# Newton's products in other slots: a two-layer non-local block on one core

## The chip, the cores and the metric

The kernel runs on one core of a Trainium2 chip. The metric is the device time of one execution in microseconds (us); three runs of the kernel before are shown with their median. TensorE is called PE here, its weight loads PEld, VectorE DVE, ScalarE ACT, GpSimd POOL and SyncE SP, as in the profile.

## The reference

Two layers of the same kind are applied to four images of 128 channels and 96 x 96 pixels, all in float32. With `C = 128` and `CI = 64`, one layer is:

```python
g_x = maxpool2(conv1x1(x, g_w, g_b)).reshape(b, CI, -1).transpose(0, 2, 1)
theta_x = conv1x1(x, theta_w, theta_b).reshape(b, CI, -1).transpose(0, 2, 1)
phi_x = maxpool2(conv1x1(x, phi_w, phi_b)).reshape(b, CI, -1)
attn = jax.nn.softmax(jnp.einsum('bqc,bck->bqk', theta_x, phi_x), axis=-1)
y = jnp.einsum('bqk,bkc->bqc', attn, g_x).transpose(0, 2, 1).reshape(b, CI, H, W)
W_y = conv1x1(y, W_w, W_b)
inv = bn_gamma * jax.lax.rsqrt(bn_var + BN_EPS)
return W_y * inv[None, :, None, None] + (bn_beta - bn_mean * inv)[None, :, None, None] + x
```

Each image has 9216 queries and 2304 keys.

## The kernel before, in words

**Slots and cycles.** There are eight blocks (an image and a layer), in the order of `ORDER`: image 0 layer 0, image 1 layer 0, image 0 layer 1, image 2 layer 0 and so on. A block's queries come in nine pairs of 1024. The keys come in 18 tiles of 128, and a slot `t` of the main loop takes two of them: nine slots are a pair, 18 slots (`CYCLE`) are a cycle, and the whole is 648 slots, 0 to 647. Within a cycle a slot is called by its number `s = t % 18`.

**What one slot issues, in this order.** The scores of the first key tile (L929: eight PE instructions of 512 columns, one for each of four 64 x 64 tiles of the array and two passes) and its exponential on ScalarE (L934); then a step called *first*, if the slot has one; the scores and exponential of the second key tile; then a step called *second* (in the tables below the main loop: *middle*); the additions of both exponentials to the row sums on VectorE (L943), between them what takes a product out of PSUM; then the products with the values for the slot before (L951, sixteen instructions); then a step that *closes* the slot; last what hangs on tails (pools, the fold of the row sums: L1023 to L1030, called the turn) and on `after` (small preparation steps). All queues are in order, and the order is this program's.

**The work beside the attention.** In cycles in which the next block's keys are made (0 to 7, 9 to 16, 18 to 25 and 27 to 30) eight slots (s = 8, 9, 11, 12, 14, 17 and 2, 5 of the next cycle) have a *stage*: a product for g, phi and theta of the next block (`Unit`), as *first*, with a sum on VectorE. Slots 3 and 13 have the projection of a finished pair (`multiply`: L1105, or L1098 where it is folded; L1116 and L1124 or L1136 take it out), slots 1 and 10 of cycles 1 to 3 a theta product (L906, L914), slot 4 after an odd unit a mix. All of these, and Newton's products, use the same two PSUM banks (`two_banks`), so a product waits until what it finds there has been read. `is_free(t)` says that a slot has none of the others.

**Newton's products.** `Fold` computes two 64 x 64 matrices B, one for each layer, by 14 Newton steps. The raw weights are transposed (`steps_raw`: four steps of four 32 x 32 transposes, L171), squared and summed (`squares`: L319, L320), and `scale` (L332) and `init` make the start. A step is `half` (a product L353 into PSUM, from which VectorE makes V, L359) and `whole` (a product L375 with V, from which ScalarE makes the next X, L379). After the 14 steps there are two rounds of `product` (L391) and `residual` (L403; L409 subtracts on VectorE); the first makes B, the second mends it, and the last residual is what a check reads. `steps_last` then notes the residual and the growth and turns the result into layer 1's last weights. Pairs from number 9 on use B in their projection, from slot 103.

Before, `scale` and `init` stand in slot 16, Newton's steps in the free slots from 18 on, and each slot holds a whole step: `half` as *first* or, where the slot before closed with one, as *middle*, and `whole` as the close. The last residual stands in slot 69, `steps_last` in slots 70 to 76.

The small tiles of `Fold` lie in `spare`, one of three buffers for an image. Image index 2 (the third) is later loaded into that buffer by six DMAs on SP, in slots 97, 104, 115, 122, 133 and 140; its first readers stand in slot 164.

Of the kernel before, what the change touches and what calls it, by code (L numbers as in the profile page):

```python
# [33 lines left out]
NP = HW // PT  # L34
KB = 2
NB = NKT // KB
# [10 lines left out]
STORE = 3  # L47
DRAIN = 15
MIX = 22


FOLDS = (8, 9, 11, 12, 15), (17, 18, 20, 21, 24)
# [7 lines left out]
CYCLE = 2 * NB  # L60
# [8 lines left out]
def shifted_blocks(ctx: ExitStack, tc: tile.TileContext, x: bass.AP, layers, out: bass.AP, flag):  # L69
# [24 lines left out]
    nc = tc.nc  # L94
# [23 lines left out]
    ones = const.tile([P, CI], F32, name="ones")  # L118
# [173 lines left out]
    class Fold:  # L292
# [146 lines left out]
        def steps(self):  # L439

            low, todo = NEWTON_LOW, []
            for k in range(NEWTON):
                c = 2.0 / (1.0 + low * (2.0 - low))
                low *= c * (2.0 - low)
                todo += [self.half(k), self.whole(k, c)]
            right = lambda: self.raw[:, CI:]
            todo += [self.product("first", right, self.first), self.residual]
            todo += [self.product("mended", lambda: self.rest, self.mended), self.residual]
            return todo

        def steps_last(self):

            w = ws[1]

            def both():
                nc.scalar.copy(self.M[:CI, :], ident[:CI, :CI])
                for step in turned(self.M[CI:, :], self.B[1][:CI, :]):
                    step()

            def scaled():  # L460
                nc.vector.tensor_scalar(self.M_bn, self.M, w.inv, None, ALU.mult)

            return [self.note, self.note_growth, both, scaled] + turned_twice(w, self.M_bn)
# [829 lines left out]
    def then(t, step):  # L1293
        after[t] = after.get(t, []) + [step]

    fold = Fold()
# [14 lines left out]
    then(9, lambda: ws[1].load_gphi((nc.sync, nc.sync)))  # L1311
    then(9, lambda: ws[1].load_theta(nc.sync))
    for i, step in enumerate(fold.steps_raw()):
        then((14, 14, 15, 15)[i], step)
    then(15, fold.keys_side)
    then(15, fold.squares)
    slow = [CYCLE + i // len(PREPARE) * CYCLE + PREPARE[i % len(PREPARE)] for i in range(11)]
    parts_of(ws[1], "gphi", slow[:4])
    parts_of(ws[1], "theta", slow[4:6])
# [25 lines left out]
    for n in range(1, len(blocks)):  # L1345
        for u in (1, 3):
            mixes[(n - 1) * NP * NB // CYCLE * CYCLE + u * CYCLE + MIX] = (n, u)
    loads = {
        5 * CYCLE + 7 + i // 2 * CYCLE + i % 2 * 7: (2, i) for i in range(6)
    } | {  # L1350
        14 * CYCLE + 14 + (i + 1) // 2 * CYCLE - i % 2 * 7: (3, i) for i in range(6)
    }
# [6 lines left out]
    def is_free(t):  # L1359
        q, s = 2 * (t // CYCLE), t % CYCLE  # L1360
        return not (
            t in stages or t in mixes or t in keys or t - 1 in keys or t in (THETAS, THETAS + 1)
            or (0 < q < NP - 1 and s in ALONE) or (q and s in PROJECT)
        )

    firsts, middles, closes = {}, {}, {}
    todo, t = fold.steps(), CYCLE
    middles[CYCLE - 2], closes[CYCLE - 2] = fold.scale, fold.init
    while todo:
        if is_free(t):  # L1370
            (middles if t - 1 in closes else firsts)[t] = todo.pop(0)
            closes[t] = todo.pop(0)
        t += 1
    for i, step in enumerate(fold.steps_last()):
        then(t + i, step)
    assert t + i + 1 < min(loads)

    gone, pending = [], (None, None)
    for t in range(total + 1):
# [8 lines left out]
        if t in keys:  # L1388
            n, i = keys[t]
# [19 lines left out]
        if t < total:  # L1409
# [12 lines left out]
            if t in loads:  # L1422
                b, i = loads[t]
# [335 lines left out]
def nonlocal_blocks(tc: tile.TileContext, x: bass.AP, layers, out: bass.AP):  # L1759
    with tc.tile_pool(name="flag", bufs=1) as pool:  # L1760
        flag = pool.tile([1, 1], I32, name="flag")
        shifted_blocks(tc, x, layers, out, flag)
        bad = tc.nc.values_load(flag[0:1, 0:1])
        with tc.If(bad > 0):
            general_blocks(tc, x, layers, out)
# [30 lines left out]
```

## Time and profile before

| what | us |
|---|---|
| median of three runs | 2479.27 |
| lowest and highest of them | 2479.05, 2481.05 |
| the profiled execution | 2479.74 |
| its span, first to last instruction | 2477.9 |
| PE busy | 2455.1 (99%) |
| DVE busy | 2073.5 (84%) |
| ACT busy | 1695.8 (68%) |
| POOL busy | 901.3 (36%) |

The mean granted clock of TensorE is 0.997. A row of a timeline has start, duration, engine, line, operation, tiles and count, and in brackets the engine's idle time before it with what ended it. Rows of the groups have busy time and mean ns behind the first bar, idle time behind the second. Rows of the waits have the total, the number and the longest. Rows of the windows have the length, then the busy time of PE, PEld, DVE, ACT and POOL, then the granted clock, the DMA share and GB/s. Matmuls overlap and their ends are modelled, so the distance of starts says more than the duration.

### The profile page before, as it was taken

Reading aid. Unit: us, or ns where it says so; the run is one execution under the profiler, and the core shown is the slowest. Engines: PE = TensorE matmul, PEld = TensorE weight load, DVE = VectorE, ACT = ScalarE, POOL = GpSimd, SP = SyncE. Lnnn points to the kernel's source line nnn. Section 1 sums busy time; section 2 is a strip of 40 time slices with the busy share of each in tenths; the row PEclk is TensorE's granted clock in tenths of the full one; section 3 lists DMA queues with packets and bytes.
Section 4 is the critical chain, followed back from the end, with each engine's and each line's share of the span. In section 5 each row is a group of like instructions: output and inputs, shape, how many; then the busy total and the mean of one; then the engine's idle time right before and its main releaser. Section 6 shows DMA issues by size and latency. Waiting matters only on the chain.

```text
span 2477.9 us, 59287 instructions
## 1 busy us (share of the span) xinstructions
PE 2455.1 (99%) x23627; PEld 1133.7 (46%) x23627; DVE 2073.5 (84%) x2671; ACT 1695.8 (68%) x1928; POOL 901.3 (36%) x1033
## 2 busy tenths in 40 slices
PE   9899999999999999999999999999999999999999
PEld 3344444454444444444444444444444444444444
DVE  8888898888788888888878888888887888887777
ACT  6566666667767667666666767677666676776666
POOL 0222332443243443434434344443433444322331
PEclk9999999999999999999999999999999999999999
DMA  5455556677467776767656677676745677644443
GB/s 189 78 91 92 99 108 130 124 141 132 81 99 132 121 135 128 138 131 140 116 101 110 124 129 134 119 137 112 123 80 99 119 125 129 126 88 86 85 87 65
DMA packets 199629, 283.95 MB, mean 115 GB/s; under 512 B 36262, under 2 KB 131888, under 8 KB 199344
## 3 DMA queue, kind: packets, MB, share of 16 engines
q0 software_dynamic: 101872, 137.69, 42.1%
q1 hardware_dynamic: 97304, 142.31, 20.1%
q8 instruction: 188, 3.08, 0.5%
q14 instruction: 97, 0.79, 0.1%
q10 hardware_dynamic: 168, 0.07, 0.0%
HBM read 54.07 MB, written 35.68 MB: 36 GB/s over the span
## 4 chain that ended last, share of the span: by engine, by line
PE 92%; DVE 4%; DMA 1%; issue 1%; ACT 0%; POOL 0%; DVEq 0%; SPq 0%; POOLq 0%; ACTq 0%
PE sc L929 43%; PE av L951 43%; PE unit_ps L693 4%; DVE sum L943 2%; PE W_ps L1098 1%; DMA sums<-x 1%; PE gphi_ps L550 1%; PE unit_ps L702 0%; DMA turned<-sum 0%; PE W_ps L1105 0%; ACT exp L934 0%; DMA sum<-turned 0%; PE mix_ps L852 0%; PE theta_ps L906 0%; DMA x<-in_x_dram 0%
## 5 line engine op out<-in xcount | busy, mean ns | idle before, releaser
L934 ACT ACTIVATE exp<-sc,nshift 128x1024 f32<-128x1024 f32 x1296 | 1400.3, 1113 | 702.0 <-PE sc L929 646.3
L943 DVE TENSOR_TENSOR sum<-sum,exp 128x1024 f32<-128x1024 f32 x1151 | 1406.6, 1222 | 300.2 <-ACT exp L934 249.2
L929 PE MATMUL sc<-theta,phi 64*64 64x512 f32 x10224 | 1533.7, 590 | 0.0
L951 PE MATMUL av<-exp,gT 64*64 64x512 f32 x10368 | 1443.0, 590 | 0.0
L929 PEld LDWEIGHTS sc<-theta,phi 64*64 64x64 f32 x10224 | 554.5, 133 | 582.3 <-issue 536.4
L951 PEld LDWEIGHTS av<-exp,gT 64*64 64x64 f32 x10368 | 542.3, 133 | 582.2 <-issue 539.6
L662 POOL DMA_DIRECT2D sums<-x x252 | 344.1, 1863 | 408.5 <-PE unit_ps L693 245.3
L1003 POOL DMA_DIRECT2D turned<-sum x140 | 115.3, 943 | 653.0 <-DMA turned<-sum 441.9
L1016 POOL DMA_DIRECT2D sum<-turned x280 | 266.5, 1729 | 118.1 <-DMA sum<-turned 115.5
L1120 POOL DMA_DIRECT2D x<-halves x122 | 109.0, 1107 | 246.8 <-ACT halves L1116 224.1
L693 PE MATMUL unit_ps<-sums,mixed 64*64 64x384 f32 x896 | 178.6, 486 | 0.2 <-DMA sums<-x 0.2
L1129 POOL DMA_DIRECT2D x<-halves x122 | 163.5, 1883 | 0.3 <-issue 0.3
L941 DVE TENSOR_TENSOR sum<-exp,exp 128x1024 f32<-128x1024 f32 x72 | 88.1, 1224 | 42.2 <-ACT exp L934 42.1
L1085 POOL DMA_DIRECT2D halves<-halves x70 | 98.4, 1406 | 0.3 <-issue 0.2
L958 ACT COPY halves<-av 128x1024 f32<-128x1024 f32 x71 | 71.9, 1013 | 32.9 <-PE av L951 31.3
L693 PEld LDWEIGHTS unit_ps<-sums,mixed 64*64 64x64 f32 x896 | 64.6, 133 | 55.1 <-issue 35.5
L693 PE MATMUL unit_ps<-x,mixed 64*64 64x384 f32 x448 | 86.4, 485 | 0.0
L1124 ACT ACTIVATE halves<-W_ps,ends 128x256 f32<-128x256 f32 x122 | 62.3, 560 | 2.0
L1098 PE MATMUL W_ps<-halves,fold 64*64 64x256 f32 x488 | 58.2, 376 | 0.0
L693 PE MATMUL unit_ps<-sums,gphiT 64*64 64x384 f32 x224 | 55.4, 493 | 0.7 <-DMA sums<-x 0.7
L662 POOL DMA_DIRECT2D sums<-sums x28 | 23.2, 830 | 81.7 <-PE unit_ps L702 38.9
L1116 ACT ACTIVATE halves<-halves,ends 128x512 f32<-128x512 f32 x61 | 49.4, 810 | 0.0
(194 smaller groups left out, 1103.8 us busy)
## 6 DMA issues: line engine op xcount, KB each, us to landing
sums<-x POOLq DMA_DIRECT2D x252, 192.0 KB, 5.8
x<-halves POOLq DMA_DIRECT2D x244, 128.0 KB, 4.6
sums<-x SPq DMA_DIRECT2D x112, 192.0 KB
turned<-sum SPq DMA_DIRECT2D x140, 128.0 KB
turned<-sum POOLq DMA_DIRECT2D x140, 128.0 KB, 3.9
halves<-halves POOLq DMA_DIRECT2D x70, 256.0 KB, 5.2
halves<-row SPq DMA_DIRECT2D x140, 128.0 KB
out_dram<-x SPq DMA_DIRECT2D x35, 512.0 KB
```

What stands on the lines that cost most here:

```text
L662: return lambda: nc.gpsimd.dma_start(out=dst(), in_=src(), accum_op=ALU.add)
L693: nc.tensor.matmul(bank[ts(c, CI), :UN], lhsT=lhsT, rhs=rhs[:, c, :], start=True, stop=True)
L929: nc.tensor.matmul(ps[ts(c, CI), ts(h, QT)], lhsT=self.blk.keys_of(k, c, h), rhs=self.th[ts(h, CI), :], start=True, stop=True,)
L934: nc.scalar.activation(e, ps, AF.Exp, bias=nshift)
L941: nc.vector.tensor_add(self.sum, self.es[0], e)
L943: nc.vector.tensor_add(self.sum, self.sum, e)
L951: nc.tensor.matmul(self.av[ts(h, CI), ts(r, QT)], lhsT=self.blk.gT[ts(r, CI), k, :], rhs=e[ts(r, CI), ts(h, QT)], start=(k == 0), stop=(k ...
L1003: nc.gpsimd.dma_start(out=self.turned[ts(h, CI)], in_=self.sum[ts(h, CI), ts(h, QT)], accum_op=ALU.add,)
L1016: nc.gpsimd.dma_start(out=folded()[ts(i, SQ)], in_=self.turned[ts(i, SQ), ts(k, n)], accum_op=ALU.add,)
L1085: nc.gpsimd.dma_start(out=self.y, in_=self.halves[:, QT:], accum_op=ALU.add)
L1120: nc.gpsimd.dma_start(out=here[:CI, h, :], in_=top[ts(h, CI), :], accum_op=ALU.add)
L1129: nc.gpsimd.dma_start(out=here[CI:, :, ts(c, n)], in_=self.y[ts(c, CI), :].rearrange("p (h n) -> p h n", h=2), accum_op=ALU.add,)
```

## The change

`steps_raw` moves from slots 14, 14, 15, 15 to 16, 17, 18, 19; `keys_side` and `squares` from 15 to 20; `scale` and `init` to slot 22. Newton's steps follow in the free slots from 24. `half` is always *middle* now. Where the slot is number 6 or 15 of a cycle (`APART`), `whole` is the *first* of the next slot, 7 or 16; elsewhere it closes the same slot. This gives the steps slots 24/25, 33/34, 36, 42/43, 51/52, 54, 58, 60/61, 69/70, 72, 73, 78/79, 82 and 87/88; the first check (`first`, `residual`) has slot 90 and the second (`mended`, `residual`) slot 91. In slot 94 a product of one column by one (`together`) with 128 rows is new. `steps_last` moves to slots 95 to 101. The loads of image index 2 move by a cycle, to slots 115, 122, 133, 140, 151 and 158.

```diff
+APART = (6, 15)
...
+        def together(self):
+            self.begin("together")
+            nc.tensor.matmul(
+                self.pss[0][:1, :1], lhsT=ones[:, :1], rhs=ones[:, :1], start=True, stop=True
+            )
...
-        then((14, 14, 15, 15)[i], step)
-    then(15, fold.keys_side)
-    then(15, fold.squares)
+        then(16 + i, step)
+    then(20, fold.keys_side)
+    then(20, fold.squares)
...
-        5 * CYCLE + 7 + i // 2 * CYCLE + i % 2 * 7: (2, i) for i in range(6)
+        6 * CYCLE + 7 + i // 2 * CYCLE + i % 2 * 7: (2, i) for i in range(6)
...
-    todo, t = fold.steps(), CYCLE
-    middles[CYCLE - 2], closes[CYCLE - 2] = fold.scale, fold.init
+    todo, t = fold.steps(), CYCLE + 4
+    middles[t], closes[t] = fold.scale, fold.init
     while todo:
+        t += 1
         if is_free(t):
-            (middles if t - 1 in closes else firsts)[t] = todo.pop(0)
-            closes[t] = todo.pop(0)
+            middles[t] = todo.pop(0)
+            if t % CYCLE in APART:
+                t += 1
+                assert is_free(t)
+                firsts[t] = todo.pop(0)
+            else:
+                closes[t] = todo.pop(0)
+    assert t < (NP + 2) * NB + 4
+    while not is_free(t + 1):
         t += 1
+    firsts[t + 1] = fold.together
     for i, step in enumerate(fold.steps_last()):
-        then(t + i, step)
-    assert t + i + 1 < min(loads)
+        then(t + 2 + i, step)
+    assert t + i + 3 < min(loads)
```

## The prediction

> **What bounds the kernel now.** I read the page first, then TensorE's timeline slot by slot, then the waits of the stretch in which something besides matmuls shows.
>
> ```profile
> PE 2455.1 (99%) x23627; PEld 1133.7 (46%) x23627; DVE 2073.5 (84%) x2671; ACT 1695.8 (68%) x1928; POOL 901.3 (36%) x1033
> ```
>
> TensorE (PE) is the bound, so a change pays only where PE stands still. Full speed comes from two neighbouring rows; the next fence has them, with the starts of slots 16, 18 and 76 and the largest hole.
>
> ```profile
> 80.96 1.90 PE L929 MATMUL sc<-theta,phi 64*64 64x512 f32 x16
> 90.02 0.27 PE L332 MATMUL fold_ps_scale<-x_spare,ones 64*64 64x2 f32 x2 [7.17 <-DVE x_spare L320]
> ...
> 98.88 1.12 PE L929 MATMUL sc<-x_spare,phi 64*64 64x512 f32 x8
> ...
> 111.25 1.90 PE L929 MATMUL sc<-x_spare,phi 64*64 64x512 f32 x16
> 112.96 1.04 PE L1105 MATMUL W_ps<-halves,WT 64*64 64x512 f32 x8
> ...
> 340.56 0.59 PE L929 MATMUL sc<-theta,phi 64*64 64x512 f32 x1
> ```
>
> Sixteen matmuls of 512 columns take 112.96 - 111.25 = 1.71 us, 0.107 each; I scale other widths by columns. A slot without extras (32 such) is 3.43 us, one with a stage (8 of 384 more) 4.08, one with eight more of 512 is 4.29. Next, the groups of PE from slot 16 to slot 75, with their counts:
>
> ```profile
> L951 PE MATMUL av<-exp,gT 64*64 64x512 f32 x961 | 119.4, 597 | 0.0
> L929 PE MATMUL sc<-theta,phi 64*64 64x512 f32 x816 | 107.5, 596 | 0.0
> L929 PE MATMUL sc<-x_spare,phi 64*64 64x512 f32 x144 | 18.6, 591 | 0.0
> L693 PE MATMUL unit_ps<-sums,mixed 64*64 64x384 f32 x108 | 17.4, 489 | 0.0
> L693 PE MATMUL unit_ps<-x,mixed 64*64 64x384 f32 x52 | 8.6, 501 | 0.0
> L1105 PE MATMUL W_ps<-halves,WT 64*64 64x512 f32 x56 | 8.1, 595 | 1.0 <-DVE stage L792 1.0
> L906 PE MATMUL theta_ps<-x,thetaT 64*64 64x512 f32 x48 | 6.4, 589 | 0.0
> ...
> L375 PE MATMUL fold_ps_half<-x_spare 64*64 64x64 f32 x112 | 5.1, 232 | 4.9 <-DVE x_spare L359 4.7
> L693 PE MATMUL unit_ps<-sums,gphiT 64*64 64x384 f32 x24 | 4.9, 482 | 0.0
> ```
>
> 2025 of 512 columns (217.2 us), 184 of 384 (14.8), 112 of 64 and small groups left out here (3.8) make 235.8 us of work. The stretch lasts 340.56 - 80.96 = 259.6. So 23.8 us are lost there, and this is all that the change can reach directly. They split so: slots 16 and 17 last 98.88 - 80.96 = 17.92 for 3.43 + 4.08 of work: 10.4 lost. The projection of slot 75 (L1105) waits for L792: 1.0 by its row, 1.5 with the second bank that waits behind the first (estimate). What is left, 11.9, stands in Newton's slots 18 to 70; the waits of weight loads and of PE in that stretch name the main ones:
>
> ```profile
> PEld fold_ps_half L375 <- DVE x_spare L359: 11.8, 8, 3.3
> ```
>
> ```profile
> PE unit_ps L702 <- DVE x_spare L409: 1.4, 1, 1.4
> ```
>
> The second product of a step (L375) waits for the update V (L359), which stands in VectorE's queue behind row sums, pools and the fold's turn. Everywhere a late VectorE is what PE waits for.
>
> **The change, part by part.** VectorE is a queue, so I walk it with durations from its timeline:
>
> ```profile
> 81.23 1.72 DVE L171 STREAM_TRANSPOSE x_spare<-x_spare 32x32 f32<-32x32 f32 x8
> 82.98 2.56 DVE L943 TENSOR_TENSOR sum<-sum,exp 128x1024 f32<-128x1024 f32 x2
> 85.45 0.44 DVE L1023 STREAM_TRANSPOSE turned<-sum 128x256 f32<-128x256 f32 x1
> ...
> 87.24 1.75 DVE L171 STREAM_TRANSPOSE x_spare<-x_spare 32x32 f32<-32x32 f32 x8
> ...
> 98.05 0.55 DVE L774 TENSOR_TENSOR stage<-stage,unit_ps 128x384 f32<-128x384 f32 x1
> ...
> 100.03 1.22 DVE L943 TENSOR_TENSOR sum<-sum,exp 128x1024 f32<-128x1024 f32 x1
> 101.16 0.22 DVE L267 TENSOR_TENSOR x_spare<-x_spare 128x64 f32<-128x64 f32 x1
> ...
> 102.18 0.47 DVE L359 SCALAR_TENSOR_TENSOR x_spare<-fold_ps_half,ident 64x64 f32<-64x64 f32 x2
> ...
> 106.79 0.69 DVE L914 TENSOR_TENSOR theta<-theta,theta_ps 128x512 f32<-128x512 f32 x1 [0.36 <-ACT theta L923]
> ...
> 108.53 0.68 DVE L1090 TENSOR_TENSOR halves<-halves 128x512 f32<-128x512 f32 x1
> ...
> 111.61 1.14 DVE L792 SCALAR_TENSOR_TENSOR stage<-unit_ps,cols_first,stage 128x384 f32<-128x384 f32 x2
> ```
>
> So two additions take 2.47 (82.98 to 85.45), one before other work 1.13 (100.03 to 101.16), the turn 1.79 (85.45 to 87.24), one step of `steps_raw` 0.87 (half of 1.75), stage 5's sums 1.98, `make_shift` 1.0, V 0.47, L914 0.6, L1090 0.6, a pool about 0.5 (estimate, a little under L774).
>
> *Raw transposes, squares, first product moved (slots 14-16 to 16-22).* Gone: the 10.4 of slots 16 and 17, that is the wait of 7.17 and 3.2 of slow running behind it. What comes: without the eight transposes at 81.23 VectorE begins slot 15's additions there, and after 2.47 + 1.79 slot 16's at 85.5, 4.5 behind the slot's start. Slot 16 adds 2.47 + 0.5 + 0.87 against 3.43 of PE (4.95 behind), slot 17 1.13 + 1.98 + 1.13 + 1.0 + 0.87 against 4.08 (7.0), slot 18 1.13 + 0.5 + 0.87 against 3.43 (6.1). In slot 19 L914 then ends 6.1 + 1.13 + 0.69 = 7.9 after the start; it frees the banks of slot 20's stage, due at 4.29 + 0.86 = 5.15. PE waits 2.8. The rest of slot 19 (addition, L1090, pool, two steps of four transposes) leaves VectorE 7.5 behind slot 20; with one addition and L792 it frees the banks for slot 21's W at 9.75, due at 4.08 + 2.8 + 1.72 = 8.6: 1.2 more. New cost 4.0. Bounds: 0 if VectorE catches up unseen, 7.2 if the hole merely moves. The squares are ready before slot 22; ScalarE's six copies end about when slot 21's exponentials start, hidden by the same wait.
>
> *Products apart in slots 6 and 15 of a cycle.* The first now follows both scores, so it no longer meets banks held by the slot before; the second comes after the next slot's first scores, so V has 1.72 + 0.86 instead of 1.72, and stands ahead of the turn, not behind it. The rows for slots 42 and 34:
>
> ```profile
> 169.22 0.34 PE L375 MATMUL fold_ps_half<-x_spare 64*64 64x64 f32 x8 [0.78 <-DVE x_spare L359]
> 198.13 1.22 PE L929 MATMUL sc<-theta,phi 64*64 64x512 f32 x8
> ...
> 202.91 0.34 PE L375 MATMUL fold_ps_half<-x_spare 64*64 64x64 f32 x8 [0.66 <-DVE x_spare L359]
> ```
>
> V lets L375 go 4.78 after slot 42's start. The new due time is 3.54 + 0.86 = 4.40: 0.35 left there, the same at slot 79 (like slot 43 it follows an odd unit's transposes), 0.15 at slot 25; 0.85 together, between 0 and today's wait. Slots 33/34, 51/52, 60/61, 69/70, 87/88: VectorE is earlier, 0.
>
> *The others (both products in one slot, the second at its end).* In slot 0 of a cycle V follows stage 5's sums. VectorE no longer gets the breathing space that slot 34's wait (0.78 by PE's row, about 1.1 against full speed) and slot 33's (0.5) give it today; it arrives later by that at slot 36. I take 1.2 there (bounds 0 and 1.6), 0.35 each at 54 and 72, 0.2 at 90. Slots 58, 73, 82: 0.
>
> *One check a slot, ended in slot 91.* The second residual's subtraction queues behind two additions and L1090, about 5.9 after slot 91's start; the next slot's stage needs its bank at 4.5. Cost 1.4, which is what L702 waits for L409 today, so that wait moves rather than goes. (0 to 2.0.)
>
> *`steps_last` from slots 70-76 to 95-101.* Same VectorE work; slot 75's 1.5 goes, slot 102 may get 0.4 (0 to 1.5).
>
> *The 128-row product.* Rows at such borders:
>
> ```profile
> 18.25 1.46 PE L550 MATMUL gphi_ps<-x,gphiT 128*64 128x512 f32 x6
> 19.63 1.09 PE L929 MATMUL sc<-theta,phi 64*64 64x512 f32 x8
> ...
> 2463.15 2.01 PE L951 MATMUL av<-exp,gT 64*64 64x512 f32 x16
> 2465.09 0.64 PE L969 MATMUL den_last_ps<-sum,ones 128*32 128x256 f32 x8
> ```
>
> Six matmuls of 0.214 are 1.28, the next starts after 1.38: 0.1 for leaving. Sixteen of 1.71 and the 0.12 by which tiles lag leave 0.1 for entering. With the product itself 0.3 (0.2 to 0.5). It levels the four tiles; what is queued behind it, slot 94's second scores and stage 95, keeps its order.
>
> *Image 3 a cycle later.* Six DMAs on SP of 768 KB move from slots 97-140 to 115-158: two leave a cycle with unit sums, two enter cycle 8, which has none; nothing else is queued with them that PE reads there. The tile's first reader is in slot 164. 0 (plus or minus 1.2).
>
> **Sum.** 4.0 + 0.85 + 2.1 + 1.4 + 0.4 + 0.3 = 9.05 new against 23.8 lost now: 14.75 saved. The profiled execution took 2479.74 (span 2477.9), so 2464.99; the median of the runs shown is 0.47 lower: 2464.5.
>
> **Rivals.** *A slow clock behind slot 20.* After the 7.17 us hole the granted clock fell:
>
> ```profile
> 82.00:90.00 8.00, 0.85 (x8) 0.00 (x0) 7.37 (x24) 2.29 (x7) 0.00 (x0) 0.74 0.02 3
> 90.00:96.00 6.00, 5.98 (x34) 3.21 (x38) 3.80 (x8) 1.69 (x5) 0.00 (x0) 0.50 0.14 45
> ```
>
> The clock (0.74, 0.50) stands before the last two columns. My 2.8 us hole lies below 7.17 and above 0.78, which did no harm. If it trips the clock, 3.2 more: 2467.7. The Trainium skill (TensorE: Matmul & The Clock Gate, Part 1) has the clock halved after an idle window of about 3.4 us, and a busy one of that length to lift it. By that rule 2.8 is too short, and 6 us at 0.50 are longer than the rule allows; the sum by it stays 2464.5.
>
> *The products do not profit.* If VectorE is late again by as much, Newton's slots keep 11.9 - 1.75 (slot 62's part) = 10.1, and new are 4.0 + 1.4 + 0.4 + 0.3: 16.2 against 23.8, so 2471.7. For it speaks VectorE's 84%; against it that V overtakes the turn.
>
> *Levelled tiles save the wait of every unit cycle.* Over the whole run:
>
> ```profile
>   ACT halves L1124: 18.7, 45
> ```
>
> Weights of the fifth product group wait for ScalarE's L1124, two banks a cycle, 0.42 each by this row; the second starts inside the first's shadow, so about 0.3 a cycle reaches PE (estimate). If level tiles avoid it in the 23 cycles with units behind slot 94, 7 more are saved: 2457.5. Against: ScalarE's own time ends it, and that does not move.
>
> *Slower.* The single 128-row product leaves the tiles in a state in which every later group of four 512-column matmuls takes longer. 553 slots of eight groups: at 3.3 ns a group the gain is gone, from 4.5 ns on the kernel is slower by over 0.2%; at 6 ns it takes 2491. Against: slot 21 (the 111.25 row) comes after the prologue's 128-row products, and a group takes 1.71 / 4 = 0.428 there, as everywhere.
>
> **How the numbers follow.** Forecast 0.65 (its own range 2461.5 to 2467.5), slow clock 0.10, no profit 0.12, levelled 0.08, slower or nothing 0.05. Leaving out the last two and small tails, the range is 2460 to 2472. About 0.2% (5 us) is what a measurement can tell from no change: faster 0.93, same 0.04, slower 0.03.
>
> **What would show it.** No 7 us hole before L332 and clock 1.0 around 90 us; L693 waiting about 2.8 for L914 near slot 20; L375 waiting under 3 in all; L693 waiting 1.4 for L409 behind the last check; slots after 94 as long as before. Wrong if VectorE's lag at slots 17 to 21 is much above 7.5, or if cycles from 6 on change length.

## The result, and the profile after

| | before | after |
|---|---|---|
| median, us (five runs each) | 2479.05 | 2465.37 |
| lowest and highest | 2477.76, 2481.05 | 2464.49, 2467.10 |
| the profiled execution, and its span | 2479.74, 2477.9 | 2464.86, 2462.7 |
| mean granted clock | 0.997 | 1.000 |

The ratio is 0.9945 with a 95% interval of 0.9931 to 0.9960: 13.7 us faster, against a forecast of 2464.5. In the code after, lines of `Fold` stand one line further down and those behind `together` (L454) seven further down: V is L360, the second product L376, the scores L936, the stages L700, the pair's projection L1112, `theta_alone`'s sum L921.

First the page's line of engines, of after:

```profile
PE 2450.6 (100%) x23629; PEld 1153.6 (47%) x23629; DVE 2072.2 (84%) x2671; ACT 1694.0 (69%) x1928; POOL 901.1 (37%) x1033
```

VectorE's work is the same. TensorE's idle time shrank, from 22.8 us (2477.9 - 2455.1) to 12.1, and its busy time by 4.5. About 3 of these are the slow running behind the hole: eight scores take 1.98 us at a clock of 0.50 (the row of e2 below) and 1.04 at 1.00. The windows of after at the place of the old hole (clock ahead of the last two columns):

```profile
82.00:90.00 8.00, 8.00 (x80) 2.91 (x76) 7.58 (x15) 4.85 (x5) 0.94 (x1) 1.00 0.31 61
90.00:96.00 6.00, 6.00 (x60) 2.14 (x56) 5.81 (x16) 4.88 (x6) 0.00 (x0) 1.00 0.28 76
```

PE is busy for 14.00 of 14 us at a clock of 1.00; before it was busy for 6.83 of them, at 0.74 and 0.50. Then PE's timeline from slot 20 (95.76) to the scale in slot 22:

```profile
95.76 1.04 PE L936 MATMUL sc<-x_spare,phi 64*64 64x512 f32 x8
96.62 0.80 PE L700 MATMUL unit_ps<-sums,mixed 64*64 64x384 f32 x2
99.48 0.55 PE L700 MATMUL unit_ps<-sums,mixed 64*64 64x384 f32 x3 [2.06 <-DVE theta L921]
...
105.20 1.18 PE L1112 MATMUL W_ps<-halves,WT 64*64 64x512 f32 x5 [0.56 <-DVE stage L799]
...
109.54 0.22 PE L333 MATMUL fold_ps_scale<-x_spare,ones 64*64 64x2 f32 x2
```

The scale product no longer waits, and the two new waits stand where the queue's walk had put them. VectorE's rows of after show the lag itself, at the first additions of slots 16, 18, 19 and 20 (which start at 80.53, 88.04, 91.47 and 95.76):

```profile
85.10 2.54 DVE L950 TENSOR_TENSOR sum<-sum,exp 128x1024 f32<-128x1024 f32 x2
...
95.02 1.23 DVE L948 TENSOR_TENSOR sum<-exp,exp 128x1024 f32<-128x1024 f32 x1
...
97.61 1.22 DVE L950 TENSOR_TENSOR sum<-sum,exp 128x1024 f32<-128x1024 f32 x1
...
103.39 1.22 DVE L950 TENSOR_TENSOR sum<-sum,exp 128x1024 f32<-128x1024 f32 x1
```

Last, the waits of PE and of weight loads from 80 to 480 us (total, number, longest), of after; the third fence has PE's own wait for V in before, from slot 16 to slot 75:

```profile
PE unit_ps L700 <- DVE theta L921: 2.1, 1, 2.1
PE unit_ps L700 <- DVE x_spare L410: 1.0, 1, 1.0
PE W_ps L1112 <- DVE stage L799: 0.6, 1, 0.6
PE fold_ps_half L354 <- DVE stage L785: 0.4, 1, 0.4
```

```profile
...
PEld fold_ps_half L376 <- DVE x_spare L360: 5.4, 6, 1.0
...
```

```profile
PE fold_ps_half L375 <- DVE x_spare L359: 4.7, 4, 2.5
```

L376's weights waited 11.8 before, 3.3 at most, and now 5.4, 1.0 at most; most of it lies beside PE's other work. In PE's own rows the wait for V was 4.7, and after has none. Where the time went is best seen by stretches. For each slot I take the distance between the starts of its first scores and of the next slot's, less the work in it at full speed (about 0.1073 us for 512 columns, a 32nd of a plain slot). The level of the sums hangs on the last digit of that price, the differences between before and after hardly do. The sums, in us, of these profiles:

| lost in slots | before | after |
|---|---|---|
| 16 to 75 | 23.95 | 6.92 |
| 76 to 103 | -0.17 | 2.46 |
| 104 to 143 | 3.19 | 1.84 |
| 144 and on | 6.66 | 7.32 |

So 14.4 of the 15.2 by which the span fell come from slots 16 to 103, the rest from the next 40 slots and from small differences of single executions on either side.

### The profile page after: what moved, and what is told of

Read it like the earlier page. It is cut to its first block, busy times and chain, and to the rows that moved or that the text cites. A ratio compares the mean times of both kernels' runs of the same rounds, so it can differ in the third digit from the quotient of the medians.

```text
span 2462.7 us, 59291 instructions
## 1 busy us (share of the span) xinstructions
PE 2450.6 (100%) x23629; PEld 1153.6 (47%) x23629; DVE 2072.2 (84%) x2671; ACT 1694.0 (69%) x1928; POOL 901.1 (37%) x1033
## 4 chain that ended last, share of the span: by engine, by line
PE 95%; DVE 3%; DMA 1%; issue 1%; ACT 0%; POOL 0%; DVEq 0%; POOLq 0%; SPq 0%; ACTq 0%
PE sc L936 44%; PE av L958 44%; PE unit_ps L700 4%; DVE sum L950 1%; PE W_ps L1105 1%; PE gphi_ps L557 1%; PE unit_ps L709 0%; DMA turned<-sum 0%; PE W_ps L1112 0%; DMA sums<-x 0%; DMA sum<-turned 0%; PE mix_ps L859 0%; DVE gT L875 0%; ACT exp L941 0%; PE theta_ps L913 0%
## 5 line engine op out<-in xcount | busy, mean ns | idle before, releaser
L936 PE MATMUL sc<-theta,phi 64*64 64x512 f32 x10224 | 1521.8, 589 | 0.0
L936 PEld LDWEIGHTS sc<-theta,phi 64*64 64x64 f32 x10224 | 561.3, 133 | 570.5 <-issue 518.7
L958 PEld LDWEIGHTS av<-exp,gT 64*64 64x64 f32 x10368 | 548.8, 133 | 570.2 <-issue 518.0
L669 POOL DMA_DIRECT2D sums<-x x252 | 339.0, 1825 | 391.6 <-PE unit_ps L700 227.2
L700 PE MATMUL unit_ps<-sums,mixed 64*64 64x384 f32 x896 | 177.5, 485 | 3.7 <-DVE theta L921 2.1
L700 PEld LDWEIGHTS unit_ps<-sums,mixed 64*64 64x64 f32 x896 | 65.0, 133 | 60.3 <-issue 35.8
L700 PE MATMUL unit_ps<-x,mixed 64*64 64x384 f32 x448 | 84.9, 483 | 0.0
L700 PE MATMUL unit_ps<-sums,gphiT 64*64 64x384 f32 x224 | 54.8, 493 | 0.0
```

Of the source, the lines that this page charges most:

```text
L669: return lambda: nc.gpsimd.dma_start(out=dst(), in_=src(), accum_op=ALU.add)
L700: nc.tensor.matmul(bank[ts(c, CI), :UN], lhsT=lhsT, rhs=rhs[:, c, :], start=True, stop=True)
L936: nc.tensor.matmul(ps[ts(c, CI), ts(h, QT)], lhsT=self.blk.keys_of(k, c, h), rhs=self.th[ts(h, CI), :], start=True, stop=True,)
L958: nc.tensor.matmul(self.av[ts(h, CI), ts(r, QT)], lhsT=self.blk.gT[ts(r, CI), k, :], rhs=e[ts(r, CI), ts(h, QT)], start=(k == 0), stop=(k ...
```

## The experiments

The theory: PE waits for a late VectorE. The change takes away the hole of the scale product, with the slow clock behind it, and most waits for V; it pays with shorter waits for the same queue. The rivals put the gain elsewhere: into the 128-row product that levels the tiles (the four 64 x 64 parts of the array, which can run at different times), into the moved loads, or into one of the two moves alone.

**e1, no 128-row product.**

```diff
-    firsts[t + 1] = fold.together
```

> The changed kernel without the 128-row product in slot 94; all else as in it (2465.37 us). Theory (PE waits for a late VectorE, the product is only a price): slot 94 becomes a plain slot of 3.43 us and 0.53 is saved, so 2464.8; cycles 10 and later keep their lengths. Rival (the product levels the four tiles and thereby saves waits): they come back behind slot 94, at least the 0.3 us a cycle of the 24 unit cycles if it holds for all of them, so 2472; if it only holds for the eight slots in which the trace shows the tiles level, under 1 us, so about 2465.5.

Measured: 2465.62 us (2463.64 to 2467.04), span 2462.1; the forecast of 0.5 less did not show in the median. Timelines of slots 94 and 95, first of after, then of e1:

```profile
394.23 1.29 PE L936 MATMUL sc<-theta,phi 64*64 64x512 f32 x8
395.45 0.19 PE L454 MATMUL fold_ps_together<-ones 128*1 128x1 f32 x2
395.57 1.09 PE L936 MATMUL sc<-theta,phi 64*64 64x512 f32 x8
396.48 1.90 PE L958 MATMUL av<-exp,gT 64*64 64x512 f32 x16
```

```profile
394.14 2.15 PE L936 MATMUL sc<-theta,phi 64*64 64x512 f32 x16
395.86 2.15 PE L958 MATMUL av<-exp,gT 64*64 64x512 f32 x16
```

Sixteen matmuls last 2.15 where three tiles run about 0.26 behind the first, and 1.90 behind the product, which brings them level. From 394.23 to 396.48 is 2.25, against 1.72 in e1: the product costs 0.53. Being level gains little: in e1 slot 102 loses 0.42 more and slot 104 0.17 less than in after, and by slot 104 the tiles of after stand 0.46 apart again. The large form of the rival (2472) falls. Its small form (under 1 us, about 2465.5) fits: 0.4 comes back at slot 102. Whether that is because the tiles are level, or because the 0.53 that PE spends lets VectorE catch up, is not shown. By the medians the product makes no difference.

**e2, only the scale's work moved.**

```diff
-        then((14, 14, 15, 15)[i], step)
-    then(15, fold.keys_side)
-    then(15, fold.squares)
+        then(16 + i, step)
+    then(20, fold.keys_side)
+    then(20, fold.squares)
...
-    todo, t = fold.steps(), CYCLE
-    middles[CYCLE - 2], closes[CYCLE - 2] = fold.scale, fold.init
+    todo, t = fold.steps(), CYCLE + 4
+    middles[t], closes[t] = fold.scale, fold.init
+    t += 2
```

> The kernel before with only the scale's work moved: raw transposes at slots 16 to 19, key sides and squares at 20, scale at 22, Newton in the old packing from slot 24 (last check in slot 72, the last steps in 73 to 79), loads where they were. Theory: the hole before the scale product goes (10.4), the new waits of slots 20 and 21 come (4.0), slot 18 is free of its 0.4, and Newton's slots keep their waits, so 2479.05 - 6.8 = 2472.3 (2470.5 to 2474). Rival (the spacing of Newton's products carries nearly all): 2479 to 2476. Rival (all of the gain is the hole): 2465 to 2467.

Measured: 2477.48 us (2474.27 to 2478.75), ratio 0.9993 (0.9984 to 1.0002). That lies in the range of the wrong rival, so the trace has to say why. Its slots 16 to 75 lose 17.1, that is 6.8 less than before, the sum that the theory has. In part that is luck: slot 75's 1.5 went too, and slots 24 and 61 lose 1.0 and 0.3 more, neither of which was in the forecast. But slots 80 and 81, which lost nothing before, lose 4.6. The row of PE there in e2, then VectorE's and ScalarE's rows ahead of it, then two windows:

```profile
355.30 1.98 PE L929 MATMUL sc<-theta,phi 64*64 64x512 f32 x8 [2.58 <-ACT exp L934]
```

```profile
344.53 1.55 DVE L868 STREAM_TRANSPOSE gT<-stage 32x576 f32<-32x576 f32 x2
346.10 0.84 DVE L171 STREAM_TRANSPOSE WT<-x_spare 32x32 f32<-32x32 f32 x4
...
349.54 1.56 DVE L868 STREAM_TRANSPOSE gT<-stage 32x576 f32<-32x576 f32 x2
...
352.93 0.85 DVE L171 STREAM_TRANSPOSE WT<-x_spare 32x32 f32<-32x32 f32 x4
```

```profile
353.81 0.30 ACT L290 COPY WT<-WT 64x128 f32<-64x128 f32 x1 [5.21 <-DVE WT L171]
354.13 2.12 ACT L934 ACTIVATE exp<-sc,nshift 128x1024 f32<-128x1024 f32 x2
```

```profile
351.60:355.01 3.41, 1.12 (x11) 0.15 (x3) 3.21 (x9) 1.17 (x2) 0.00 (x0) 1.00 0.08 13
355.01:358.42 3.41, 3.12 (x20) 1.24 (x24) 3.10 (x4) 2.74 (x5) 0.00 (x0) 0.50 0.26 77
```

With Newton three slots later the last steps stand in 73 to 79. Their transposes (L171) meet those of an odd unit (L868) and the fold's turn, so the second four end at 353.8. The copy of their result (L290), the end of `steps_last`, stands in ScalarE's queue ahead of the next exponentials. ScalarE stands idle for 5.21 us until the copy can run, and PE waits for the exponential behind it. The clock is then at 0.50 for 3.41 us. A step that I had costed at nothing, `steps_last`, has a price that depends on its slot, and it is paid in two queues.

**e7, e2 with the last steps where the change has them.**

```diff
-        then(t + i, step)
+        then(95 + i, step)
...
-        5 * CYCLE + 7 + i // 2 * CYCLE + i % 2 * 7: (2, i) for i in range(6)
+        6 * CYCLE + 7 + i // 2 * CYCLE + i % 2 * 7: (2, i) for i in range(6)
```

> The kernel with only the scale's work moved (2477.5 us), but its last steps in slots 95 to 101, as in the changed kernel, instead of 73 to 79, and image 3 a cycle later, which that needs. Newton's packing is the old one. Theory (the scale alone gave only 2 because the last steps ran into the transposes of the odd unit: slots 80 and 81 lost 4.6 there): these 4.6 go, nothing over 0.5 comes at 95 to 102, so 2472.9 (2471.5 to 2474). Rival (slots 80 and 81 are late through Newton's steps themselves): 2477, unchanged.

Measured: 2474.10 us (2472.18 to 2476.47), ratio 0.9977 (0.9967 to 0.9986), span 2472.9; slots 76 to 103 lose 0.0. So the last steps were the cause in e2. The median lies 1.2 above the forecast, just outside its range. In the profiled execution (2474.82) two places stand out against e2: slot 122, which loses 1.6 more and varies from run to run (see e4), and slot 44. PE's row at the head of slot 44 and the clock around it in e7, and the clock in e2 around the same wait of slot 43 (2.5 there as well, from 200.31 to 202.78):

```profile
202.68 0.34 PE L375 MATMUL fold_ps_half<-x_spare 64*64 64x64 f32 x8 [2.46 <-DVE x_spare L359]
```

```profile
199.91:203.33 3.42, 0.95 (x20) 0.32 (x16) 3.19 (x9) 0.88 (x3) 0.00 (x0) 1.00 0.36 58
203.33:206.74 3.41, 3.41 (x28) 1.92 (x24) 2.84 (x3) 1.25 (x3) 0.00 (x0) 0.50 0.23 77
```

```profile
198.00:201.41 3.41, 2.31 (x28) 0.77 (x20) 3.28 (x6) 2.60 (x4) 0.82 (x1) 1.00 0.33 52
201.41:204.83 3.42, 2.05 (x30) 1.19 (x34) 3.19 (x7) 1.10 (x3) 0.00 (x0) 1.00 0.09 15
```

In e7 slot 44 runs at 0.50 for 3.41 us and loses 1.7, half of that; in e2 it loses nothing. The section on the hardware says what differs.

**e3, only the packing changed.**

```diff
+APART = (6, 15)
...
-    todo, t = fold.steps(), CYCLE
+    todo, t = fold.steps(), CYCLE - 1
...
     while todo:
+        t += 1
         if is_free(t):
-            (middles if t - 1 in closes else firsts)[t] = todo.pop(0)
-            closes[t] = todo.pop(0)
-        t += 1
+            middles[t] = todo.pop(0)
+            if t % CYCLE in APART:
+                t += 1
+                assert is_free(t)
+                firsts[t] = todo.pop(0)
+            else:
+                closes[t] = todo.pop(0)
...
-        then(t + i, step)
+        then(t + 1 + i, step)
```

> The kernel before with only the packing of Newton's products changed (first and second apart in slots 6 and 15 of a cycle, from slot 18 on, checks end in slot 88, the last steps in 89 to 95); raw, squares and scale at 14 to 16 and loads as before, no 128-row product. Theory: the hole of 10.4 stays; of the 13.4 lost in slots 18 to 75 remain 0.4 (18), 0.6 (24, 25), 1.3 (36), 0.4 each at 43 and 54, 0.6 each at 72 and 79, together 4.3, so 2479.05 - 9.1 = 2469.9 (2468.5 to 2472). Rival (VectorE is late again, the products don't profit): 2476 to 2479. In both the projection in slot 75 should no longer wait 1.5, as the last steps are gone from there.

Measured: 2470.42 us (2470.01 to 2472.36), ratio 0.9966 (0.9954 to 0.9978). PE's waits of e3 from 60 to 480 us:

```profile
PE fold_ps_scale L333 <- DVE x_spare L321: 7.2, 1, 7.2
PE fold_ps_half L354 <- DVE stage L779: 0.4, 1, 0.4
PE unit_ps L694 <- DVE x_spare L410: 0.4, 1, 0.4
PE fold_ps_half L376 <- DVE x_spare L360: 0.3, 1, 0.3
...
```

The hole is untouched, and PE's waits for V (L376) are down from 4.7 to 0.3 us. That the products do not profit is ruled out. Slots 83 and 93 lose 0.7 and 1.1, which the forecast did not have; the last steps stand around slot 93. The two moves together: 9.1 here and 5.5 in e7 (each against the executions of before beside it) are 14.6, of which the 1.5 of slot 75, gone in both, counts once: 13.1, against 13.7 for the whole change.

**e4, only image 3 loaded later.** The edit is the second of e7's, alone.

> The kernel before with only image 3 loaded a cycle later. Theory (the loads stand beside the units' sums on the DMA engines): the wait in slot 122 drops from 1.8 to the 0.6 that every unit cycle has, slots 140 and 143 lose 0.6 each of theirs, slot 125 gets 0.9, so 2479.05 - 1.4 = 2477.7. Rival (nothing on PE's path): 2479.05, within 0.3. Rival (the loads carry a large part of the change): below 2475.

Measured: 2479.21 us (2477.22 to 2481.34), ratio 0.9999 (0.9990 to 1.0008). The profiled run is 1.2 shorter, by slot 122 (1.0 lost, 1.8 before) and slots 140 and 143; the median does not follow, so the forecast of 1.4 was a miss. Slot 122 waits for the units' sums from memory, and its loss varies among all these kernels' profiles from 0.6 to 2.1, and once 4.6, so one profile cannot price the loads. They carry no large part.

**e6 and e9, the hole filled.** Into `scale` of the kernel before, ahead of its own products (e9 has `range(6)`):

```diff
             self.begin("scale")
+            for _ in range(12):
+                for c in range(2):
+                    for r in range(2):
+                        nc.tensor.matmul(
+                            self.pss[r][ts(c, CI), :], lhsT=ident[ts(r, CI), ts(r, CI)],
+                            rhs=xs[0][ts(r, CI), :QT], start=True, stop=True,
+                        )
```

> The kernel before with 48 products of 512 columns added in slot 16, ahead of the scale's; their results are overwritten and used nowhere. They fill 5.1 of the 7.2 us in which TensorE stands idle there. Theory (the slow running of slots 16 and 17 comes from the idle hole): the granted clock stays at 1.0 from 82 to 96 us, the scale product still starts near 90, and 3.2 of the 10.4 go: 2476.3 (2475.5 to 2477.5). Rival (the slow running comes from something else, queues or memory): clock 0.5 as before and 2479.5; if the added products also come in the way, 2480 to 2484.

Measured: 2480.72 us (2477.60 to 2482.20), ratio 1.0005 (0.9995 to 1.0015). I had mis-sized the filling: each product is two instructions of 0.107, so it ran for 10.3 us and held the scale product back from 90.0 to 92.5. The forecast (2476.3) was missed. Yet the clock stayed at 1.00, and what the delay cost came back behind it.

> The kernel before with 24 products of 512 columns added ahead of the scale's in slot 16 (their results are overwritten and used nowhere). The run with 48 showed that a product of that shape is two instructions of 0.107 each, so that 48 took 10.3 us and held the scale product back by 2.5; 24 take 5.1 and end before VectorE's sums do. Theory (slow running behind the hole comes from the idle time): clock 1.0 from 82 to 96 us, the scale product near 89.6 as before, the stretch from it to slot 18 takes 5.9 instead of 8.9, so 3.0 are saved: 2476.4 (2475.5 to 2477.8). Rival (the short rest of the hole, about 2 us, trips the clock too): 2478 to 2480.

Measured: 2476.07 us (2474.04 to 2479.45), ratio 0.9989 (0.9980 to 0.9998). PE's timeline of e9 at slot 16 and its window behind the hole:

```profile
82.27 5.33 PE L333 MATMUL fold_ps_scale<-x,ident 64*64 64x512 f32 x48
89.62 0.22 PE L339 MATMUL fold_ps_scale<-x_spare,ones 64*64 64x2 f32 x2 [2.02 <-DVE x_spare L320]
...
95.49 1.12 PE L936 MATMUL sc<-x_spare,phi 64*64 64x512 f32 x8
```

```profile
90.00:96.00 6.00, 6.00 (x62) 3.31 (x56) 5.87 (x12) 3.27 (x5) 0.94 (x1) 1.00 0.27 60
```

From the scale product to slot 18 it takes 95.49 - 89.62 = 5.87, against 98.88 - 90.02 = 8.86 before. Useless work in the hole saves 3.0 us there (2.6 by the medians): that much of the 10.4 was the slow clock.

**e5, raw transposes where VectorE stands idle.**

```diff
-        then(16 + i, step)
+        then(8 + i, step)
```

> The changed kernel with the four steps of raw transposes at slots 8 to 11, where VectorE stands idle for 0.2, 1.3, 1.4 and 0.9 us in its trace, instead of 16 to 19; all else as in it (2465.4 us). Theory (slots 20 and 21 wait because 3.5 us of transposes push VectorE's queue back): three steps of 0.87 leave the queue ahead of L921, so the wait in slot 20 falls from 2.6 to 0, that of slot 21 from 1.4 to 0.3 or less; at most 0.5 comes new in slots 9 to 13; 2461.9 (2461 to 2463). Rival (the wait is L921's own, behind ScalarE or the row sums): 2465.4, unchanged.

Measured: 2462.46 us (2461.71 to 2463.37), ratio 0.9932 (0.9915 to 0.9948). PE's wait of e5 from 85 to 115 us:

```profile
PE unit_ps L700 <- DVE theta L921: 0.2, 1, 0.2
```

2.06 has become 0.2; slots 20 and 21 lose 0.75 and 0.42 instead of 2.61 and 1.40 (the forecast was 0 and at most 0.3), and nothing is lost in slots 9 to 13. The wait for L921 was VectorE's queue, not L921.

**e8, four edits at once.** Beside e5's edit and without the product:

```diff
-    then(32, ws[1].make_shift)
+    then(39, ws[1].make_shift)
...
-            todo += [self.product("mended", lambda: self.rest, self.mended), self.residual]
+            todo += [self.product("mended", lambda: self.rest, self.mended)]
...
+        def checked(self):
+            self.begin("checked")
+            self.residual()
...
+        then(97 if i == 0 else 94 + i, step)
+    middles[96] = fold.checked
```

> The changed kernel with four edits: raw transposes at slots 8 to 11; no 128-row product; the second layer's shift at slot 39 instead of 32 (its ends split in 44 and 45); the second check a product of its own in slot 96, with its note in 97 and the other last steps in 95 to 100. Theory, by its waits: 3.7 from slots 20 and 21, 0.5 from slot 94, 1.0 of the 1.3 in slot 36, 1.2 of the 1.3 in slot 92, against up to 0.5 new at 97 and 102: 2465.4 - 5.9 = 2459.5 (2458 to 2461.5). Rival (waits only move along to the next late place): 2463 or more.

Measured: 2461.19 us (2460.07 to 2465.87, four runs), ratio 0.9933 (0.9916 to 0.9949), span 2458.0 against 2462.7 of after. All of PE's waits in e8 from 80 to 480 us:

```profile
PE unit_ps L704 <- DVE stage L749: 0.2, 1, 0.2
PE unit_ps L704 <- DVE theta L925: 0.2, 1, 0.2
```

Slot 36 loses 0.36 instead of 1.26, slot 92 nothing instead of 1.29, slot 94 nothing instead of 0.53; slots 102 and 48 give 0.84 and 0.3 back.

**e10, more of it still earlier.**

```diff
-        then(8 + i, step)
+        then((4, 8, 9, 9)[i], step)
...
-    parts_of(ws[0], "W", (11, 12, 13, 17))
+    parts_of(ws[0], "W", (10, 11, 12, 12))
```

> The kernel with the four edits (2461.2 us, span 2458.0) with still more of VectorE's work in its early idle time: raw transposes at slots 4, 8, 9, 9 and the first layer's W steps with the shift at 10, 11, 12, 12 instead of 11, 12, 13, 17. Theory: the rest of the waits in slots 20 and 21, 0.74 and 0.43, goes, and nothing over 0.3 comes in slots 9 to 14: span 2456.9, time 2459.5 (2458 to 2461). Rival (VectorE has no room left before slot 13 and stages 8 to 12 wait): 2461 or more.

Measured: 2460.83 us (2459.96 to 2463.22), ratio 0.9922 (0.9909 to 0.9936). Slots 20 and 21 lose nothing now, but slot 12 loses 0.9: the room ahead of slot 13 is used up, and 1.2 was exchanged for 0.9. Its profile is that of its slowest run, and slot 122 alone lost 4.6 there. PE's rows at that place in e10, and the clock around them:

```profile
498.55 0.83 PE L704 MATMUL unit_ps<-sums,mixed 64*64 64x384 f32 x2 [1.23 <-ACT exp L945]
499.97 0.51 PE L704 MATMUL unit_ps<-sums,gphiT 64*64 64x384 f32 x1 [0.59 <-DMA sums<-x]
```

```profile
497.03:500.44 3.41, 1.58 (x12) 0.55 (x13) 1.96 (x3) 1.46 (x2) 0.92 (x2) 1.00 0.70 107
500.44:503.85 3.41, 3.41 (x23) 2.21 (x19) 1.95 (x4) 0.99 (x1) 3.41 (x7) 0.50 0.99 333
```

All runs of e5 and of e10 lie below the lowest of after, and so do three of e8's four. They ran beside other executions of the kernel before than after did, and the intervals of the ratios overlap; that e5 and e10 are faster than after is likely, the order among e5, e8 and e10 stays open.

## Why the prediction was right

The mechanism held, and not only the number: PE waits for a late VectorE, and the lag of that queue could be summed from its rows.

*The hole.* The 10.4 of slots 16 and 17 went as said, and e9 confirms the share of the clock (3.0 for 3.2).

*Slots 20 and 21.* The walk through VectorE's queue gave 2.8 and 1.2; 2.61 and 1.40 were lost. L921 ends 7.9 after slot 19's start, as the walk had it (slot 19 starts 4.29 ahead of the 95.76 row, and VectorE's next work starts at 99.35). The lag behind the starts of slots 16, 18, 19 and 20 was summed as 4.5, 7.0, 6.1 and 7.5; VectorE's rows give 4.57, 6.98, 6.14 and 7.63.

*Products apart.* 33/34, 51/52, 60/61, 69/70 and 87/88 are free of loss, as forecast, and slot 43 loses 0.36 for 0.35. Under-sized were 24/25 (0.62 for 0.15: the first product there waits 0.4 for L785, a bank that I had taken as free) and 79 (0.58 for 0.35). Together 1.56 for 0.85.

*Both products in one slot.* Slot 36 lost 1.26 for 1.2, 54 0.36 for 0.35, 72 0.56 for 0.35, 90 0.15 for 0.2: 2.3 for 2.1. The 1.2 was taken between wide bounds, not summed. e8 shows whose work was late there: `make_shift`, four slots ahead, is the 0.9 by which slot 36 stands above the others (e1 and e5, which leave it in slot 32, keep 1.3). That the waits of slots 33 and 34 used to cover it, as the prediction argued, fits before, where slot 36 lost 0.4 with the same `make_shift`.

*The check.* 1.29 for 1.4: the wait moved from slot 62 to slot 92, now for L410.

*The last steps.* 0 lost at slot 102 for 0.4 (0.4 in e1, without the 128-row product). But the step "same VectorE work; slot 75's 1.5 goes" was right by its place, not by its reasoning: e2 shows that the same work in slots 73 to 79 costs 4.6.

*The 128-row product.* The term was mis-sized, 0.53 for 0.3, just outside its bounds of 0.2 to 0.5.

In all, slots 16 to 103 still lose 9.4 where the sum said 9.05; terms too small by 0.7 (apart), 0.2 and 0.2 stand against terms too large by 0.4 and 0.1, so that the total is nearer than its parts. *The loads* were put at 0, plus or minus 1.2; e4's median differs by 0.3.

*The rivals.* e3 disposes of "the products do not profit". "Levelled tiles" fell by e1, and cycles from 10 on lose the 0.3 that they lost before, as level tiles did not last beyond slot 103. "Slower" fell with the result: later groups are as long as before. "A slow clock behind slot 20" did not happen here, and that was partly luck: 2.46 was enough in e7, so the rival was nearer than the 0.10 argued from 2.8 us.

*The signs.* The hole is gone and the clock is 1.0; slots after 94 are as long as before. L693's waits for L914 and L409 are 2.1 and 1.0 in PE's rows (for 2.8 and 1.4; the slots lose 2.6 and 1.3). "L375 waiting under 3 in all" holds for PE, which does not wait for V any more, and not for the weight loads' row from which the prediction read 11.8: there 5.4 are left.

## What to carry to other kernels

Where the bounding engine waits, look at which queue is late and walk that queue slot by slot with durations from its rows; the place and size of waits that do not exist yet can then be forecast to some tenths of a microsecond. Cheap preparation steps belong where that queue shows idle time, and their price depends on the slot, so a moved step has to be walked at its new place even if its work is unchanged, and in every queue in which it has an instruction. A wait of TensorE of 2 us or more can cost more than its length (1.7 us more in e7), because the granted clock may fall behind it.

## What the runs showed of the hardware

Behind waits of about 2.5 us the granted clock sometimes falls and sometimes does not: it was 0.50 for 3.41 us behind 2.46 in e7 and around the end of 2.58 in e2, and 1.00 behind the same slot 43 wait in e2. The traces show a reason. In each of them the clock changes only at instants that lie whole multiples of 3.413 us apart (in before at 7.35, 85.86, 96.10 and 2475.19, which are 23, 3 and 697 of them), at another phase in each profile (the first at 7.35 in before, 6.68 in after, 5.35 in e7). Before's rows around its hole, cut at these instants, and one around its slot 43 wait (2.47 us, from 206.79 to 209.26):

```profile
82.44:85.86 3.42, 0.41 (x4) 0.00 (x0) 3.26 (x6) 0.16 (x1) 0.00 (x0) 1.00 0.00 0
85.86:89.27 3.41, 0.00 (x0) 0.00 (x0) 3.10 (x15) 1.08 (x5) 0.00 (x0) 0.50 0.02 4
89.27:92.68 3.41, 2.66 (x18) 1.38 (x22) 2.76 (x6) 2.17 (x4) 0.00 (x0) 0.50 0.25 77
92.68:96.10 3.42, 3.42 (x24) 1.93 (x20) 1.67 (x6) 0.34 (x1) 0.00 (x0) 0.50 0.02 5
205.32:208.74 3.42, 1.47 (x16) 0.40 (x8) 3.20 (x8) 1.79 (x2) 0.82 (x1) 1.00 0.36 54
```

What fits is the idle time within one such stretch, not the length of the wait. The clock fell behind stretches of 3.41 us that were idle for 3.0 (before), 2.5 (e7) and 2.3 (e2) of it, and stayed behind 1.95 (the last row). In e2 slot 43's wait is cut into 1.1 and 1.4 by the end of a stretch, in e7 it lies within one; after's 2.06 at slot 20 is cut into 1.4 and 0.65. In e10 a stretch with only 1.8 idle was enough, in two waits of which the longer is 1.23. Between these only two matmuls ran, so idle time may not be all that counts, and no run settles where the limit is. The clock came back behind a stretch in which PE was busy for 3.4 (before, e7) or 3.1 (e2), not behind one with 2.7 (the third row).

The Trainium skill (TensorE: Matmul & The Clock Gate, Part 1) asks for an idle window of about 3.4 us and says that the window runs freely, so that its phase varies from run to run. The traces agree with the second and not with the first: 2.46 was enough. So the prediction's "longer than the rule allows" was a misreading: the 6.1 us at 0.50 from 90.0 to 96.1 are the rest of one stretch, which PE did not fill, and one that it did. That some of the several microseconds between runs of one kernel come from the phase is likely, not shown.

The four tiles of the array do not run in step: in after they stand 0.4 to 0.5 us apart in most slots behind 104, where a plain slot still takes 3.43 us, and a 128-row product of one column brings them level for 0.53 us.
